# Inverse roots of two norms: one GpSimd power in place of a seed and ten operations

## The chip, the cores and the metric

The kernel runs on one core of a Trainium2 chip. The metric is the device time of one execution in microseconds, as the median of several runs. Beside the runs there is one profiled execution, from which all durations here come. A core has five engines with a queue each: PE (TensorE, matmuls and transposes; its weight loads are listed as PEld), DVE (VectorE), ACT (ScalarE), POOL (GpSimd) and SP, which only issues DMAs here. An engine executes its instructions in the order of its queue, and waits at an instruction until the work of other engines that it needs is done.

## The reference

The input x has 512 x 512 positions of 64 channels in fp32. Two layers of the same form follow each other, and each adds its result to x. Cut to what matters:

```python
def layer(x):                                   # twice, with weights of its own
    xn = _ln(_gn(x)) * norm_scale + norm_bias   # group norm, then layer norm, over 64 channels
    left  = (xn @ Wl + bl) * mask * sigmoid(xn @ Wlg + blg)      # 64 -> 128
    right = (xn @ Wr + br) * mask * sigmoid(xn @ Wrg + brg)
    out_gate = sigmoid(xn @ Wog + bog)
    out = _banded_ingoing(left, right, 4)       # each row: sum of 9 neighbouring rows, weighted by left
    out = _ln(out) * out_gate                   # layer norm over 128 channels, with scale and bias
    return x + out @ Wo + bo                    # 128 -> 64

def _ln(x, eps=1e-6):
    m, v = mean(x, axis=-1), var(x, axis=-1)
    return (x - m) / sqrt(v + eps)

def _gn(v, G=32, eps=1e-5):                     # mean and variance of 2 channels over all positions
    return (g - m) / sqrt(s + eps)
```

So there are three places where an inverse root 1/sqrt(v + eps) is needed: the inner layer norm (one number per position), the outer layer norm (one per position) and the group norm (one per group of channels, once a layer).

## The kernel before

The 512 rows are cut into 9 blocks of up to 64 rows, which overlap by the width of the band, and the columns into two halves of 256. The 128 partitions hold the 64 rows of a block for both halves. A chunk is 128 columns of each half; a layer has 9 x 2 = 18 chunks. A chunk is walked in 16 steps, in each of which one unit `z` of 8 columns per half enters, and, some 30 steps later, one unit `Out` leaves. `layer` (with its loop over `t`, the step) writes out by hand which engine does what in which order: everything that it calls through `en` is kept in program order on its engine, by the helper at line 373, and so nearly all instructions of the profile bear line 373.

What happens to a unit that enters: `load` fetches z; `affine` applies the group norm (two operations with `ga` and `gb`, on DVE for the first units of a layer, on POOL for the others); `inner_stats` takes mean and variance with bn_stats on DVE; `solve` makes the inverse root; `inner_norm` subtracts the mean and multiplies by the root `rs` (two operations on POOL); `transposed` turns z on PE, from where ACT copies it (`zT`); `right` and `right_gate`, `right_end` make the gated right product (PE, ACT's sigmoid `sg`, DVE's multiply into `RO`).

What happens to one that leaves: in the first ten steps of a chunk `mix` multiplies `RO` with the left matrix `A` (one or two mixes a step, each of 32 matmuls), and ACT and DVE copy the result back into `RO`; `out_stats` takes its statistics on DVE; `solve` makes the root; `norm` applies it on ACT (eight operations a step, with `rs` as scale and `nm` as bias); `turned`, `gates`, `times_gate` (DVE, into `ZH`) and `end` follow; `biased` adds the bias to the fetched x in `XR` on POOL, and `ended` adds the result and stores it. In the first layer `sums` gathers the statistics for the second layer's group norm.

`solve` is called once every four steps, for the inner norm of about four units and the outer norm of four others at once. DVE forms the variances of both in one tile `v` of up to 96 columns (in most solves 32 + 32), and the negative means `nm`; `rsqrt` makes the roots into `r`; two POOL operations multiply the outer roots by the mask and `nm` by the roots. `rsqrt(o, v, vec, e)` makes a seed on `vec` by treating the float's bits as an integer (one tensor_scalar into `o`), and refines it on `e` in two rounds: six and four operations, of which the profile shows the results as `rsqrt` (the two scratch tiles) and `rs` (`o`).

In the order of the step in which it runs, `solve` stands behind the step's `affine` and statistics and ahead of `right_end`, `biased` and `times_gate`. So on POOL it is followed by the XR addition of the same step and the z of the next; on DVE by the product that frees a pair of PSUM banks for PE.

The group norm's roots come from `group_affine`, which calls `rsqrt(ga, ve)` with both engines left at their default, DVE: once after the statistics of the input (`input_stats`), and once between the layers, at the end of `mid_stats`.

Of the kernel before, what the change touches and what calls it, by code (L numbers as in the profile page):

```python
# [8 lines left out]
F32 = mybir.dt.float32  # L9
I32 = mybir.dt.int32  # L10
AF = mybir.ActivationFunctionType
ALU = mybir.AluOpType
# [4 lines left out]
P = 128  # L17
# [11 lines left out]
NB = 32  # L29
# [50 lines left out]
def tile_two_banded_layers(  # L80
# [6 lines left out]
    nc = tc.nc  # L87
# [7 lines left out]
    const = ctx.enter_context(tc.tile_pool(name="const", bufs=1))  # L95
    sm = ctx.enter_context(tc.tile_pool(name="sm", bufs=2))
# [28 lines left out]
        same.rearrange("p (g t) -> p g t", t=2), last(pair, 2), 1.0 / (2.0 * L * L), None, ALU.mult  # L125
    )

    def one_bank():
        return ps.tile([P, 512], F32, tag="ps", name="bank")

    def two_banks():
        return ps2.tile([P, 1024], F32, tag="ps2", name="banks")

    def rsqrt(o: bass.AP, v: bass.AP, vec=nc.vector, e=nc.vector):


        p, n = v.shape
        t, u = (
            sm.tile([P, 3 * NB], F32, tag=f"rsqrt{i}", name="rsqrt", bufs=1)[:p, :n]
            for i in range(2)  # L140
        )
        vec.tensor_scalar(
            o.bitcast(I32), v.bitcast(I32), -0.5, float(0x5F3759DF), ALU.mult, ALU.add
        )
        e.tensor_tensor(t, o, o, ALU.mult)
        e.tensor_tensor(t, t, v, ALU.mult)
        e.tensor_scalar(u, t, -10.0 / 3.0, None, ALU.add)
        e.tensor_tensor(t, t, u, ALU.mult)
        e.tensor_scalar(t, t, 5.0, None, ALU.add)
        e.tensor_tensor(o, o, t, ALU.mult)  # L150
        e.tensor_tensor(t, o, o, ALU.mult)
        e.tensor_tensor(t, t, v, ALU.mult)
        e.tensor_scalar(t, t, -27.0 / 1024.0, 0.5625, ALU.mult, ALU.add)
        e.tensor_tensor(o, o, t, ALU.mult)


    PARTS = (
# [61 lines left out]
    def solve_layer(i: int, f: dict, r: dict, tmp, half: bass.AP):  # L219
# [9 lines left out]
        for nm, lo, hi in (("right", 0, 2), ("left", 2, 4), ("gate", 4, 5)):  # L229
            lo, hi = lo * H, hi * H  # L230
            pm = one_bank()[:, : hi - lo]
            nc.tensor.matmul(pm, lhsT=half, rhs=aug[:, lo:hi], start=True, stop=True)
            pb = one_bank()[:, : hi - lo]
            nc.tensor.matmul(pb, lhsT=hb, rhs=raw[:, lo:hi], start=True, stop=False)
            nc.tensor.matmul(pb, lhsT=ones_row, rhs=brow[:, lo:hi], start=False, stop=True)
            nc.vector.tensor_tensor(r[nm], aug[:, lo:hi], pm, ALU.subtract)
            nc.vector.tensor_tensor(r[nm], r[nm], pb, ALU.add)
# [14 lines left out]
        nc.vector.tensor_scalar(r["Wo"], f["wo"], osc, None, ALU.mult)  # L252

        pb = one_bank()
        nc.tensor.matmul(pb[:, :D], lhsT=ones_row, rhs=f["bo"], start=True, stop=True)
        add = r["add"].rearrange("p (t c) -> p t c", c=D)
# [51 lines left out]
    def group_affine(mean: bass.AP, var: bass.AP, pool):  # L308

        ve = pool.tile([P, D], F32, name="g_ve")  # L310
        nc.vector.tensor_scalar(ve, var, GN_EPS, None, ALU.add)
        rsqrt(ga, ve)
        nc.vector.scalar_tensor_tensor(gb, mean, -1.0, ga, ALU.mult, ALU.mult)
# [284 lines left out]
    def solve(w: dict, ins: list, outs: list, sti, sto):  # L598

        ni, no = len(ins) * JU, len(outs) * JU  # L600
        v = sm.tile([P, 3 * NB], F32, tag="var", name="var", bufs=1)[:, : ni + no]
        r = sm.tile([P, 3 * NB], F32, tag="rs", name="rs", bufs=3)[:, : ni + no]
        if ni:
            en.vector.tensor_scalar(
                v[:, :ni].rearrange("p (k t) -> p k t", t=2), sti[:, : ni // 2, 2::3],
                1.0 / D, LN_EPS, ALU.mult, ALU.add,
            )
            for n, u in enumerate(ins):
                u.rs = r[:, n * JU : (n + 1) * JU]
        if no:  # L610

            js = slice(outs[0].m, outs[0].m + no)
            vo = v[:, ni:]
            en.vector.scalar_tensor_tensor(
                vo.rearrange("p (k t) -> p k t", t=2), sto[:, :, 2::3], 1.0 / H,
                w["m2"][:, js].rearrange("p (k t) -> p k t", t=2), ALU.mult, ALU.mult,
            )
            en.vector.tensor_scalar(vo, vo, LN_EPS, None, ALU.add)
            nm = sm.tile([P, NB], F32, tag="nm", name="nm")[:, :no]
            en.vector.tensor_scalar(  # L620
                nm.rearrange("p (k t) -> p k t", t=2), sto[:, :, 1::3], -1.0, None, ALU.mult
            )
        rsqrt(r, v, en.vector, en.gpsimd)
        if no:
            ro = r[:, ni:]
            en.gpsimd.tensor_tensor(ro, ro, w["m"][:, js], ALU.mult)
            en.gpsimd.tensor_tensor(nm, nm, ro, ALU.mult)
            for n, o in enumerate(outs):
                o.rs, o.nm = ro[:, n * JU : (n + 1) * JU], nm[:, n * JU : (n + 1) * JU]
# [109 lines left out]
    def layer(src: bass.AP, dst: bass.AP, w: dict, stats: bool, then=None):  # L739
# [60 lines left out]
        for t in range(min(loads), last_t + 3):  # L800
# [59 lines left out]
            if t % 4 == 0:  # L860
                st, us = sti.pop((t + 4) // 4, (None, []))
                so, os = sto or (None, [])
                sto = None
                if us or os:
                    solve(w, us, os, st, so)
# [156 lines left out]
def build(arrays):  # L1022
    import concourse.bacc as _bacc

    nc = _bacc.Bacc("TRN2", target_bir_lowering=False, num_devices=1)
    aps = {}
    for name in _INS:
        a = arrays[f"in_{name}_dram"]
        aps[name] = nc.dram_tensor(
            f"in_{name}_dram", a.shape, mybir.dt.from_np(a.dtype), kind="ExternalInput"  # L1030
        ).ap()
    out = nc.dram_tensor("out_0_dram", aps["x"].shape, F32, kind="ExternalOutput").ap()
    layers = [{n: aps[f"L{i}_conv_{n}"] for n in _NAMES} for i in range(2)]
    with tile.TileContext(nc) as tc:
        tile_two_banded_layers(tc, aps["x"], layers, out)
    return nc
# [10 lines left out]
```

## Time and profile before

| | |
|---|---|
| runs | 4804.82, 4806.53, 4807.79 us; median 4806.53 us |
| profiled execution | 4808.51 us |
| its span, from the first to the last instruction | 4806.5 us |
| granted TensorE clock, mean | 0.948 of full speed |
| set-up and statistics of the input | 0 to about 300 us |
| first layer | about 300 to 2560 us |
| second layer | about 2560 to 4806 us |

A line of a group of instructions reads: source line, engine, operation, output<-inputs by the program's names, shapes, count; then busy time in us and mean ns of one; then the idle time of the engine just before these instructions, and what ended it. In the list of waits, "A <- B: total, times, longest" means that A's engine stood idle until B was done. A line of the timeline has start and duration in us, and in square brackets the idle time before it with what ended that. A line of a stretch has its bounds, its length and the busy time of each engine with the number of instructions.

### The profile page before, as it was taken

The page shows a single profiled execution, that of the slowest core. Times are in us where ns is not written, and L with a number is a line of the kernel's source. Part 1 is how long each engine was busy: PE and PEld are TensorE (multiplying, and loading weights), DVE is VectorE, ACT ScalarE, POOL GpSimd, SP SyncE. Part 2 cuts the span into 40 slices and gives each one's busy share as a digit, 9 for nine tenths or more (in the row PEclk, how much of TensorE's full clock was granted, in tenths as well). Part 3 has the DMA queues.
Part 4 walks back from the last instruction along what each step waited for, and adds up shares of the span by engine and source line. Part 5 has one row for each costly group of instructions (what it writes and reads, how often), then busy time and mean ns, then how long its engine had stood idle before and what let it go on. Part 6 is the DMA issues. An engine that isn't in the chain of part 4 may idle for free. (4 is left out here: it accounts for less than half of the span.)

```text
span 4806.5 us, 193543 instructions
## 1 busy us (share of the span) xinstructions
PE 3796.6 (79%) x76306; PEld 3293.0 (69%) x76306; DVE 3929.9 (82%) x9635; ACT 3708.4 (77%) x8732; POOL 3817.1 (79%) x4739
## 2 busy tenths in 40 slices
PE   1025799989999999999985478888888888888888
PEld 0024688878888887888854467777777777777775
DVE  6954788888888888888867478888888888888887
ACT  0013689888888898989883268888888888888899
POOL 0035999999999999999734589999999999999964
PEclk9997999999999999999997689999999999999999
DMA  7859677777777777777763967777777777777876
GB/s 299 336 178 108 172 212 213 215 210 215 211 209 210 211 214 212 214 212 215 199 170 100 105 168 212 216 214 209 217 213 215 213 213 218 210 216 211 222 200 179
DMA packets 1437651, 983.63 MB, mean 205 GB/s; under 512 B 167202, under 2 KB 1284424, under 8 KB 1432392
## 3 DMA queue, kind: packets, MB, share of 16 engines
q1 hardware_dynamic: 1432064, 969.75, 73.6%
q8 instruction: 604, 9.90, 0.9%
q14 instruction: 303, 2.48, 0.2%
q10 hardware_dynamic: 4680, 1.50, 0.1%
HBM read 658.42 MB, written 312.46 MB: 202 GB/s over the span
## 5 line engine op out<-in xcount | busy, mean ns | idle before, releaser
L373 ACT ACTIVATE on<-RO,nm,rs 128x128 f32<-128x128 f32 x4608 | 1927.7, 496 | 15.3 <-PE bank L373 9.9
L373 PEld LDWEIGHTS banks<-pack,zT 64*128 64x128 f32 x18576 | 1251.3, 195 | 549.5 <-ACT zT L373 288.9
L373 PE MATMUL banks<-pack,zT 64*128 64x128 f32 x18576 | 1365.6, 289 | 272.8 <-ACT zT L373 222.6
L373 DVE TENSOR_TENSOR RO<-banks,sg 128x512 f32<-128x512 f32 (+1 forms) x1188 | 795.3, 673 | 228.3 <-POOL sg L373 116.2
L373 DVE SCALAR_TENSOR_TENSOR ZH<-bank,pack,gate 128x448 f32<-128x448 f32 (+1 forms) x1152 | 741.6, 685 | 173.3 <-PE bank L373 97.3
L373 ACT ACTIVATE sg<-banks 128x512 f32<-128x512 f32 (+1 forms) x1188 | 698.0, 589 | 188.6 <-PE banks L373 188.2
L373 DVE BATCH_NORM_STATS2 sto<-RO 128x6 f32<-128x256 f32 x2304 | 800.8, 411 | 3.7
L373 POOL TENSOR_TENSOR z<-z,gb 128x512 f32<-128x512 f32 x536 | 684.8, 1278 | 42.0
L373 PE MATMUL bank<-RO,A 64*64 64x128 f32 x18432 | 706.0, 292 | 3.9 <-ACT RO L373 2.4
L373 PE MATMUL bank<-pack,ZH 128*64 128x64 f32 x18432 | 694.6, 231 | 5.0 <-ACT gate L373 4.1
L373 POOL TENSOR_TENSOR z<-z,ga 128x512 f32<-128x512 f32 x536 | 685.6, 1279 | 3.2 <-DMA z<-mid_x 1.9
L373 POOL TENSOR_TENSOR z<-z,rs 128x512 f32<-128x512 f32 x586 | 619.3, 1057 | 46.0
L373 DVE COPY RO<-bank 128x512 f32<-128x512 f32 x576 | 398.4, 692 | 310.6 <-PE bank L373 307.3
L373 PEld LDWEIGHTS bank<-pack,ZH 128*64 128x64 f32 x18432 | 612.6, 143 | 47.3 <-ACT gate L373 8.5
L373 POOL TENSOR_TENSOR z<-z,sti 128x512 f32<-128x512 f32 x586 | 627.9, 1072 | 0.0
L373 PEld LDWEIGHTS bank<-RO,A 64*64 64x64 f32 x18432 | 582.0, 142 | 43.0 <-ACT RO L373 4.1
L373 ACT ACTIVATE gate<-bank 128x448 f32<-128x448 f32 (+1 forms) x1152 | 565.8, 545 | 34.5 <-PE bank L373 32.0
L373 ACT ACTIVATE zT<-banks 128x512 f32<-128x512 f32 (+1 forms) x1084 | 463.5, 481 | 139.6 <-PE banks L373 128.9
L373 PE MATMUL bank<-zg,pack 64*128 64x448 f32 (+1 forms) x2304 | 564.3, 556 | 4.6 <-DMA zg<-later 4.6
L373 ACT COPY RO<-bank 128x512 f32<-128x512 f32 x576 | 333.2, 579 | 282.3 <-PE bank L373 282.1
L373 PE MATMUL banks<-ident,z 64*128 64x64 f32 x4336 | 254.1, 233 | 359.2 <-DVE RO L373 336.9
L373 DVE BATCH_NORM_STATS2 sti<-z 128x6 f32<-128x128 f32 x2344 | 500.5, 280 | 15.2 <-POOL z L373 14.2
(144 smaller groups left out, 3908.6 us busy)
## 6 DMA issues: line engine op xcount, KB each, us to landing
later<-zT SPq DMA_DIRECT2D x576, 256.0 KB
A<-left_of SPq DMA_DIRECT2D x1152, 128.0 KB
zg<-later SPq DMA_DIRECT2D x576, 256.0 KB
z<-in_x_dram SPq DMA_DIRECT2D x576, 128.0 KB
z<-mid_x SPq DMA_DIRECT2D x576, 128.0 KB
gn_x<-in_x_dram SPq DMA_DIRECT2D x16, 4096.0 KB
XR<-in_x_dram SPq DMA_DIRECT2D x448, 112.0 KB
mid_x<-XR SPq DMA_DIRECT2D x448, 112.0 KB
```

Of the source, the lines that this page charges most:

```text
L373: return lambda *a, **k: tc.keep_in_program_order(f(*a, **k))
```

## The change

`rsqrt` loses the seed, the ten operations and their two scratch tiles. In their place stands one POOL tensor_tensor with the power operator, whose second operand is a constant column of -0.5, stretched over all columns. The column is set up once by DVE. `solve` calls it with POOL as the engine; `group_affine`, whose code stays, now gets POOL by default, where it had DVE.

```diff
@@ -125,33 +125,20 @@
+    minus_half = const.tile([P, 1], F32, name="minus_half")
+    nc.vector.memset(minus_half, -0.5)
+
...
-    def rsqrt(o: bass.AP, v: bass.AP, vec=nc.vector, e=nc.vector):
+    def rsqrt(o: bass.AP, v: bass.AP, e=nc.gpsimd):
         p, n = v.shape
-        t, u = (
-            sm.tile([P, 3 * NB], F32, tag=f"rsqrt{i}", name="rsqrt", bufs=1)[:p, :n]
-            for i in range(2)
-        )
-        vec.tensor_scalar(
-            o.bitcast(I32), v.bitcast(I32), -0.5, float(0x5F3759DF), ALU.mult, ALU.add
-        )
-        e.tensor_tensor(t, o, o, ALU.mult)
-        e.tensor_tensor(t, t, v, ALU.mult)
-        e.tensor_scalar(u, t, -10.0 / 3.0, None, ALU.add)
-        e.tensor_tensor(t, t, u, ALU.mult)
-        e.tensor_scalar(t, t, 5.0, None, ALU.add)
-        e.tensor_tensor(o, o, t, ALU.mult)
-        e.tensor_tensor(t, o, o, ALU.mult)
-        e.tensor_tensor(t, t, v, ALU.mult)
-        e.tensor_scalar(t, t, -27.0 / 1024.0, 0.5625, ALU.mult, ALU.add)
-        e.tensor_tensor(o, o, t, ALU.mult)
+        e.tensor_tensor(o, v, minus_half[:p].broadcast_to([p, n]), ALU.pow)
@@ -620,7 +607,7 @@
-        rsqrt(r, v, en.vector, en.gpsimd)
+        rsqrt(r, v, en.gpsimd)
```

## The prediction

> **What bounds the kernel now.** First the busy shares of the whole span, then the busy time of stretches inside the second layer.
>
> ```profile
> PE 3796.6 (79%) x76306; PEld 3293.0 (69%) x76306; DVE 3929.9 (82%) x9635; ACT 3708.4 (77%) x8732; POOL 3817.1 (79%) x4739
> ```
>
> ```profile
> core 0: us, PE busy (x) PEld busy (x) DVE busy (x) ACT busy (x) POOL busy (x), PEclk, DMA share, GB/s
> 3500.00:3530.00 30.00, 24.65 (x484) 21.45 (x480) 26.79 (x68) 29.83 (x74) 26.17 (x33) 1.00 0.80 225
> 3530.00:3575.00 45.00, 38.25 (x838) 33.81 (x840) 40.81 (x95) 37.20 (x89) 42.28 (x54) 0.96 0.76 210
> ```
>
> The page alone would let no engine stand out. The stretches do: a chunk of 16 steps has six steps without mixing, where ACT is full (29.83 of 30.00), and ten with it, where POOL is (42.28 of 45.00, the rest being gaps between its small operations). So I went to POOL's groups, here from 3000 to 4400 us, where 49 solves run, 28.57 us apart:
>
> ```profile
> L373 POOL TENSOR_SCALAR rsqrt<-rsqrt 128x64 f32<-128x64 f32 x147 | 48.0, 326 | 12.9
> L373 POOL TENSOR_TENSOR rs<-rs,rsqrt 128x64 f32<-128x64 f32 x98 | 31.4, 321 | 8.2
> L373 POOL TENSOR_TENSOR rsqrt<-rsqrt,var 128x64 f32<-128x64 f32 x98 | 31.3, 320 | 7.7
> L373 POOL TENSOR_TENSOR rsqrt<-rs 128x64 f32<-128x64 f32 x98 | 28.7, 293 | 29.6 <-DVE rs L373 25.8
> L373 POOL TENSOR_TENSOR rsqrt<-rsqrt 128x64 f32<-128x64 f32 x49 | 15.7, 321 | 4.1
> ```
>
> These five groups are the ten operations of a root. Busy: 48.0 + 31.4 + 31.3 + 28.7 + 15.7 = 155.1 us, 3.17 us a solve. Idle before them: 62.5 us, of which 25.8 is a wait for DVE's seed and 36.7 (0.75 a solve) dispatch gaps. So the chain holds POOL for 3.91 us, and POOL's only true slack is the wait, whose size the two layers give (1000 to 2000 us with 34 solves, 3000 to 4400 us with 49):
>
> ```profile
> POOL rsqrt L373 <- DVE rs L373: 29.3, 34, 1.9
> ```
>
> ```profile
> POOL rsqrt L373 <- DVE rs L373: 25.8, 35, 1.7
> ```
>
> That is 0.86 us a solve in layer 1 and 0.53 in layer 2: POOL is occupied for 97% and 98% of these windows. It is the engine that the pace hangs on, and a late POOL also stretches DVE, as one solve in a mixing stretch shows (timeline of DVE, then of PE):
>
> ```profile
> 3558.04 1.01 DVE L373 TENSOR_SCALAR var<-sti 128x32 f32<-128x32 f32 x1
> 3558.98 0.18 DVE L373 SCALAR_TENSOR_TENSOR var<-sto,pack 128x32 f32<-128x32 f32 x1
> 3559.19 1.20 DVE L373 TENSOR_SCALAR var<-var 128x32 f32<-128x32 f32 x1
> 3560.31 0.17 DVE L373 TENSOR_SCALAR nm<-sto 128x32 f32<-128x32 f32 x1
> 3560.43 1.23 DVE L373 TENSOR_SCALAR rs<-var 128x64 int32<-128x64 int32 x1
> 3561.58 0.68 DVE L373 TENSOR_TENSOR RO<-banks,sg 128x512 f32<-128x512 f32 x1
> ...
> 3562.40 0.46 PE L373 MATMUL banks<-ident,z 64*128 64x64 f32 x8 [3.92 <-DVE RO L373]
> ```
>
> Three operations that take 0.16 to 0.20 us in a quiet solve take 1.0 to 1.2 here, while POOL runs 1.28 us operations back to back; the product RO comes late behind them, and PE waits 3.92 us for it.
>
> **The change, part by part.** The program has 160 solves: 128 of them 64 columns wide (64 a layer), 32 between 24 and 48 wide at the ends of the layers. From each go a DVE seed and ten POOL operations; one POOL power operation comes. POOL's other work keeps its order, and no DMA moves.
>
> *Removed from POOL:* 3.91 us a solve. *Removed from DVE:* the seed, 0.20 us undisturbed, up to 1.23 as above. While POOL sets the pace this gain is worth nothing by itself, since DVE then waits for POOL's z later; if POOL were relieved it would come out of PE's waits.
>
> *Added to POOL:* a power, D us for 64 columns, plus one gap (0.75/10 = 0.08). No row shows a power. Lower bound: one two-input operation of that shape, 0.32 us. Upper bound, an estimate: a power with a free exponent is a logarithm, a product and an exponential; I count some 10 terms for the first, 6 for the last, each a multiply-add, and as many steps again to split and join exponents and sort out special values, 32 to 40 steps. As instructions of their own these would cost 0.40 us each (0.32 and a gap), so 40 x 0.40 = 16 us. The nearest row is the chain itself, ten such steps in 3.91 us. Inside one instruction the gaps and some reading and writing fall away, so I take 32 steps at 0.24, the cheapest step of the chain: 7.7, rounded to D = 8 us. A step could be far cheaper with everything kept inside the cores; both ends stay in the range.
>
> [...]
>
> *Behind it on POOL* stand the two small products for rs and nm, then XR and all z of the next steps; for these wait ACT's norm, one step later, and PE's transposes. With POOL already full, each microsecond beyond what is removed and the slack lengthens the solve's period:
>
> - layer 1: 64 x (8 + 0.08 - 3.91 - 0.86) = 64 x 3.31 = 212 us
> - layer 2: 64 x (8 + 0.08 - 3.91 - 0.53) = 64 x 3.64 = 233 us
> - the 32 narrower solves lie where POOL is idle much of the time (185.34 us busy of 260 from 300 to 560 us, 96.97 of 206 in the last stretch): 0; without that cover, half of D against 3.3 us, 32 x 0.8 = 26 us.
>
> A power holds POOL for long; could it hold DVE's small operations as the z operations do? The next of these are a period later and need z that POOL scales after the power, so they can't meet it: 0.
>
> *Group norm.* Its two roots, so far on DVE, become a power on POOL between two DVE operations. The first is covered: DVE waits 47.2 us for zeros to land before XR is cleared. The second is bare, at the seam of the layers:
>
> ```profile
> 2563.90 0.20 DVE L142 TENSOR_SCALAR ga<-on 128x64 int32<-128x64 int32 x1
> ...
> 2566.62 0.22 DVE L313 SCALAR_TENSOR_TENSOR gb<-on,ga 128x64 f32<-128x64 f32 x1
> ```
>
> Seed to gb takes 2.72 us; the power takes 8 and two hand-overs at 0.08 (seed's end to POOL's start at 3506.06): + 5.4 us. The constant's memset is one column on DVE during set-up, under 0.1 us, beside the loads.
>
> Sum: 212 + 233 + 5 = 450 us onto the span of 4806.5 (its execution 4808.5, the median of the runs 4806.53): **5257 us**. D from 6 to 11 gives 5000 to 5640, the own range of this case.
>
> **Rivals.** *A cheap power (faster).* The point that decides is D = 4.4 to 4.7 us, where the formulas cross zero. For it speaks that ten trips through memory become one; against it, the count of steps. What it would give: PE's transposes start 7.17 us apart in undisturbed steps with two mixes, 6.23 with one, 5.69 with none; the chunk from 3530.34 to 3643.98 has 6, 4 and 6 of them, 102 us undisturbed against 113.6 measured. So some 11 us a chunk, 18 chunks a layer: 200 us in layer 2; layer 1's same reckoning from 1491.62 to 1558.43 gives 7.8 a chunk, 140. All of it would be 4470; D of 1 to 2.5 frees 3 to 1.5 us a solve and brings perhaps 60%: **4600 us**. Chance 0.33.
>
> *A very dear power.* If the cores work their partitions one after another, D is 16 us and more: 64 x (11.31 + 11.64) = 1469, narrower solves 32 x 4.7 = 150, the seam 13: **6440 us** and up without end, as POOL has no cover left. Against it: each POOL row shows 128 partitions at 1.6 ns a column ((1043 - 320)/448). Chance 0.10.
>
> *Nothing happens.* D within about 0.1 us of the crossing, or the freed POOL time turns into ACT's bound, which six steps a chunk already have: **4806 us**. Chance 0.03; that the program is not what it says is excluded, since its queues hold one power a solve.
>
> **How the numbers follow.** The forecast has 0.54, the rivals 0.33, 0.10 and 0.03. No change is within 0.2% (10 us), about what a measurement of this kernel can tell. Slower: 0.54 + 0.10. The range runs from 4560, which leaves out the best part of the cheap case, to 6400, which leaves out the dear one.
>
> **What would show it.** A group rs<-var,minus_half of 128 operations at 128x64 and its mean, counted start to start: near 8 us my D holds, under 4.4 the first rival. POOL's wait for DVE before it should vanish and POOL be full in all stretches, with ACT's non-mixing steps longer than 5.69 us. Wrong would be a long power with little lost time, or a short one with PE waiting as before.

## The result, and the profile after

The changed kernel takes 5629.52 us (four runs, 5627.82 to 5631.06), the kernel before on the same chip 4805.67 us: ratio 1.1716, 95% interval 1.1695 to 1.1736. It is 17% slower; the forecast was 5257 us, within a range of 4560 to 6400. The page of the profiled execution opens with the busy shares:

```profile
PE 4045.0 (72%) x76306; PEld 3479.2 (62%) x76306; DVE 3916.1 (70%) x9454; ACT 3750.1 (67%) x8732; POOL 4875.8 (87%) x3301
```

POOL has 1438 instructions fewer than before and 1059 us more to do. DVE and ACT have hardly more, so their shares fall. (PE has the same number of matmuls, with 248 us more of busy time, at a mean granted clock of 0.889 instead of 0.948. That clock did not set the time here: of four executions of run 11 below, two had a clock of 0.87 and two of 0.89, and their times lie within 2.1 us of each other.) One stretch in each layer shows what is full:

```profile
core 0: us, PE busy (x) PEld busy (x) DVE busy (x) ACT busy (x) POOL busy (x), PEclk, DMA share, GB/s
1000.00:2000.00 1000.00, 806.02 (x16076) 703.78 (x16076) 722.10 (x1727) 747.47 (x1727) 970.77 (x665) 0.91 0.63 176
4000.00:4700.00 700.00, 524.47 (x9994) 457.31 (x9994) 504.79 (x1212) 512.53 (x1205) 678.91 (x461) 0.88 0.63 176
```

POOL is at 97%, and the gaps between its operations make up most of the rest. The groups of POOL's instructions hold what stands for the ten operations of the root:

```profile
L360 POOL TENSOR_TENSOR rs<-var,minus_half 128x64 f32<-128x64 f32 x128 | 1348.4, 10535 | 45.4 <-DVE nm L360 34.7 <-DVE var L360 9.0
...
L360 POOL TENSOR_TENSOR rs<-var,minus_half 128x32 f32<-128x32 f32 x22 | 119.3, 5424 | 100.6 <-DVE nm L360 95.9 <-DVE var L360 4.7
```

A power of 64 columns takes 10.53 us where the chain took 3.91, and one of 32 columns 5.42: 0.16 us a column. What stands behind it is seen in the timeline around one of them (all engines; lines left out between):

```profile
3996.93 10.53 POOL L360 TENSOR_TENSOR rs<-var,minus_half 128x64 f32<-128x64 f32 x1
...
4007.86 0.25 POOL L360 TENSOR_TENSOR nm<-nm,rs 128x32 f32<-128x32 f32 x1
4008.07 1.18 POOL L360 TENSOR_TENSOR XR<-XR,pack 120x512 f32<-120x512 f32 x1
4008.14 1.66 ACT L360 ACTIVATE on<-RO,nm,rs 128x128 f32<-128x128 f32 x4 [6.28 <-POOL nm L360]
...
4009.28 0.69 DVE L360 TENSOR_TENSOR XR<-bank,XR 120x512 f32<-120x512 f32 x1 [5.38 <-POOL XR L360]
...
4010.03 1.97 PE L360 MATMUL bank<-RO,A 64*64 64x128 f32 x28 [4.92 <-DVE XR L360]
```

ACT stands 6.28 us for the root, DVE 5.38 us for the XR sum behind it in POOL's queue, and PE 4.92 us for a bank that DVE frees late. Such waits are among the longest of the whole span:

```profile
ACT on L360 <- POOL nm L360: 614.7, 137, 8.9
...
DVE XR L360 <- POOL XR L360: 518.8, 131, 8.0
```

POOL's own wait for DVE, 29.3 us between 1000 and 2000 us before, has shrunk to 6.2 in the same window:

```profile
L360 POOL TENSOR_TENSOR rs<-var,minus_half 128x64 f32<-128x64 f32 x28 | 295.0, 10535 | 6.7 <-DVE nm L360 3.4 <-DVE var L360 2.8
```

### The profile page after: what moved, and what is told of

It is laid out like the page before. It is cut to its first block, busy times and chain, and to the rows that moved or that the text cites. A ratio compares the mean times of both kernels' runs of the same rounds, so it can differ in the third digit from the quotient of the medians.

```text
span 5629.0 us, 191928 instructions
## 1 busy us (share of the span) xinstructions
PE 4045.0 (72%) x76306; PEld 3479.2 (62%) x76306; DVE 3916.1 (70%) x9454; ACT 3750.1 (67%) x8732; POOL 4875.8 (87%) x3301
## 5 line engine op out<-in xcount | busy, mean ns | idle before, releaser
L360 ACT ACTIVATE on<-RO,nm,rs 128x128 f32<-128x128 f32 x4608 | 1920.3, 492 | 640.0 <-POOL nm L360 614.7
L360 PEld LDWEIGHTS banks<-pack,zT 64*128 64x128 f32 x18576 | 1372.5, 213 | 933.3 <-ACT zT L360 627.8
L360 PE MATMUL banks<-pack,zT 64*128 64x128 f32 x18576 | 1491.0, 307 | 611.4 <-ACT zT L360 569.6
L360 POOL TENSOR_TENSOR rs<-var,minus_half 128x64 f32<-128x64 f32 (+4 forms) x160 | 1535.8, 9599 | 197.0 <-DVE nm L360 141.9
L360 PE MATMUL bank<-RO,A 64*64 64x128 f32 x18432 | 751.5, 299 | 183.1 <-DVE XR L360 172.9
L360 DVE TENSOR_TENSOR XR<-bank,XR 120x512 f32<-120x512 f32 (+1 forms) x576 | 395.8, 687 | 563.3 <-POOL XR L360 518.8
L360 PEld LDWEIGHTS bank<-RO,A 64*64 64x64 f32 x18432 | 610.6, 146 | 236.6 <-DVE XR L360 183.3
L360 PE MATMUL bank<-zg,pack 64*128 64x448 f32 (+1 forms) x2304 | 628.6, 615 | 3.4 <-DMA zg<-later 3.4
L360 DVE COPY RO<-bank 128x512 f32<-128x512 f32 x576 | 397.5, 690 | 322.0 <-PE bank L360 319.1
L360 DVE BATCH_NORM_STATS2 sti<-z 128x6 f32<-128x128 f32 x2344 | 504.5, 281 | 124.6 <-POOL z L360 121.9
```

The lines of the kernel that those rows point to most:

```text
L360: return lambda *a, **k: tc.keep_in_program_order(f(*a, **k))
```

## The experiments

The runs of one group (1 to 4, 5 to 8, 9 to 11) share a chip and its runs of the kernel before (medians 4831.88, 4827.48 and 4837.55 us), so they are read by their ratio to it; "+121" means the ratio less one, times the 4806.5 us of the first trace.

**1. What a root for nearly nothing would bring.** The changed kernel's power becomes a multiplication:

```diff
-        e.tensor_tensor(o, v, minus_half[:p].broadcast_to([p, n]), ALU.pow)
+        e.tensor_tensor(o, v, minus_half[:p].broadcast_to([p, n]), ALU.mult)
```

> The changed kernel with a multiplication in the place of the power, on the same operands and at the same places of POOL's queue; the roots themselves are left out. Theory (POOL's occupancy sets the pace on both sides): one operation of about 0.32 us and a gap instead of 3.91 us, 3.5 us freed a solve, of which ACT and PE let 60 to 90% through: 4500 to 4680 us. Rival (POOL was only just full, and other engines take over at once when it is relieved): 4790 to 4810 us.

4721.20 us, ratio 0.9772 (0.9756 to 0.9788): -110 us. The gain is there, so POOL did set the pace, but it is a quarter of the 450 us of POOL time that are freed (3.5 x 128), and less than my 4600 for a cheap power. Both theories miss: POOL was the fullest engine, but the next were close behind (before, from 3000 to 4400 us: POOL busy for 93%, DVE for 89, ACT for 88). In the second layer (3000 to 4400 us) of this run:

```profile
3000.00:4400.00 1400.00, 1192.78 (x24810) 1041.30 (x24812) 1238.94 (x2998) 1260.64 (x3003) 1192.32 (x1154) 0.98 0.79 219
```

```profile
POOL XR L360 <- DMA XR<-mid_x: 124.3, 73, 5.7
```

ACT (fourth) is now at 90%, DVE at 88 and POOL at 85; and POOL, running ahead, stands 124 us for the fetch of x.

**2. Half the power.** In the changed kernel's `rsqrt`:

```diff
-        e.tensor_tensor(o, v, minus_half[:p].broadcast_to([p, n]), ALU.pow)
+        h = n // 2
+        e.tensor_tensor(o[:, :h], v[:, :h], minus_half[:p].broadcast_to([p, h]), ALU.pow)
+        e.tensor_tensor(
+            o[:, h:], v[:, h:], minus_half[:p].broadcast_to([p, n - h]), ALU.mult
+        )
```

> The power on the first half of the columns, a multiplication on the second half, whose roots are left out. Theory (occupancy, 0.16 us a column): 5.42 + 0.25 and two gaps, 5.83 us in place of 3.91: 64 x (5.83 - 3.91 - 0.86) + 64 x (5.83 - 3.91 - 0.53) = 157 us, the seam 3: 4966 us, 4930 to 5010. Rival (what costs is the lateness of the root for ACT, which before the change began 1.7 us after the end of the chain, so that the first 1.7 us are free): 64 x 2 x (5.83 - 3.91 - 1.7) = 28 us: 4825 to 4845.

4953.13 us, ratio 1.0252 (1.0237 to 1.0268): +121, against 160 by occupancy and 28 by the rival. The first stands, 40 us too high. Two rows tell most of why, POOL's group here and its wait for the seed over the whole span before:

```profile
L364 POOL TENSOR_TENSOR rs<-var,minus_half 128x32 f32<-128x32 f32 x256 | 722.1, 2837 | 11.4 <-DVE var L364 7.5
```

```profile
L373 POOL TENSOR_TENSOR rsqrt<-rs 128x64 f32<-128x64 f32 x256 | 74.9, 293 | 111.6 <-DVE rs L373 101.6
```

The two operations hold POOL for (722.1 + 3.9)/128 = 5.67 us a solve, not 5.83, and the slack is 101.6 us in all, where the two windows gave 64 x (0.86 + 0.53) = 89. With both, and the 7.5 us of waiting that are left, the wide solves come to 128 x (5.67 - 3.91) - 101.6 + 7.5 = 131 us.

**3. XR out of the power's way.** In the changed kernel's step, `biased` moves ahead of `solve`:

```diff
+            if t in outs:
+                biased(outs[t], w, stats)
             if t % 4 == 0:
                 st, us = sti.pop((t + 4) // 4, (None, []))
...
-            if t in outs:
-                biased(outs[t], w, stats)
```

> The changed kernel with the step's XR addition ahead of the power in POOL's queue instead of behind it. Theory (occupancy; the waits of DVE for XR, 519 us in the trace, only show where a full POOL makes others wait): 5590 to 5650 us, the wait moves to other lines. Rival (the long instruction hurts by standing ahead of XR, on which DVE and then PE hang): most of the 519 us come back, 5100 to 5300 us.

5658.69 us, ratio 1.1713 (1.1696 to 1.1731), the same as the changed kernel's 1.1716 (5630 us as the first chip would have it, inside the expected range). DVE's 519 us of waiting for XR are gone from the head of the list, and other waits have grown in their place (these three were 614.7, 319.1 and 121.9 us in the changed kernel):

```profile
ACT on L360 <- POOL nm L360: 699.3, 142, 10.1
DVE RO L360 <- PE bank L360: 428.7, 460, 9.9
...
DVE sti L360 <- POOL z L360: 319.1, 119, 8.5
```

The wait for XR named a victim, not the cause.

**4. A power that nobody waits for.** The kernel before keeps its roots and gets an extra power:

```diff
+    idle = const.tile([P, 2 * NB], F32, name="idle")
...
             if t in outs:
                 biased(outs[t], w, stats)
+            if t in outs and t in units and t % 4 == 0:
+                en.gpsimd.tensor_tensor(
+                    idle, all_ones[:, : 2 * NB], minus_half.broadcast_to([P, 2 * NB]), ALU.pow
+                )
```

> The kernel before with its seed and ten operations, and an extra power of 64 columns whose result nobody reads, behind the XR addition of every fourth step (64 a layer). Theory (occupancy): 64 x (10.61 - 0.86) + 64 x (10.61 - 0.53) = 1269 us more: 6075 us, 5980 to 6130. Rival (the lateness of the roots costs, not POOL's time): nothing waits for this result, 4806 to 4850 us.

6094.72 us, ratio 1.2616 (1.2597 to 1.2635): +1257 us where 1269 were worked out. Its group and POOL's remaining wait for the seed, between 1000 and 2000 us:

```profile
L377 POOL TENSOR_TENSOR idle<-all_ones,minus_half 128x64 f32<-128x64 f32 x26 | 274.6, 10561 | 0.0
...
L377 POOL TENSOR_TENSOR rsqrt<-rs 128x64 f32<-128x64 f32 x50 | 14.7, 294 | 7.9 <-DVE rs L377 6.0
```

No root is later for its own sake here, and the time is lost all the same. With runs 2 and 3 this settles that POOL's occupancy is what costs, not the lateness of the root or the long instruction's place ahead of XR.

**5. What a power's price depends on.** During set-up, in the kernel before:

```diff
+        for power in (-0.5, 2.0, 1.0):
...
+            for p, n in ((P, 64), (P, 8), (P, 128), (16, 64), (4, 64)):
+                tc.keep_in_program_order(
+                    nc.gpsimd.tensor_tensor(
+                        probe[:p, :n], base[:p, :n], ex[:p].broadcast_to([p, n]), ALU.pow
+                    )
+                )
...
```

> The kernel before, with powers of several shapes and exponents on POOL in the set-up, where POOL has nothing to do (2 to 228 us), results unread. Theory (one pass of the same code for each column, all partitions side by side, nothing depends on the values; 0.31 us and 0.16 a column by the widths of the changed kernel): 128x8 1.6 us, 128x64 10.5, 128x128 20.8, and 16x64 and 4x64 10.5 too, the same for exponents 2 and 1 and for a base of 1. Rival (partitions one after another): 4x64 about a quarter of 16x64. Rival (short ways for easy exponents): 2 and 1 far under 10.5. The kernel's time is that of before, 4806 to 4835 us.

4834.62 us in a single run, and 4827.48 before (4822.43 to 4834.08). From POOL's groups (base 1.5; L971 has the base 1.0):

```profile
L965 POOL TENSOR_TENSOR probe<-base,ex-0.5_108 128x128 f32<-128x128 f32 x1 | 20.7, 20727 | 0.1
...
L965 POOL TENSOR_TENSOR probe<-base,ex2.0_115 128x64 f32<-128x64 f32 x1 | 10.5, 10517 | 0.1
...
L971 POOL TENSOR_TENSOR probe<-base,ex1.0_122 128x64 f32<-128x64 f32 x1 | 10.5, 10517 | 0.1
...
L965 POOL TENSOR_TENSOR probe<-base,ex2.0_115 4x64 f32<-4x64 f32 x1 | 10.5, 10506 | 0.1
...
L965 POOL TENSOR_TENSOR probe<-base,ex-0.5_108 128x8 f32<-128x8 f32 x1 | 1.6, 1646 | 0.0
```

Twice the columns cost twice the time ((20.73 - 1.65)/120 = 0.159 us a column, 0.37 for the instruction). Four partitions cost what 16 and 128 do (10.51 to 10.73 us at 64 columns), so the partitions are not taken one after another. An exponent of 1 or 2 or a base of 1 is no cheaper. Both rivals fall.

**6. The power for the group norm alone:** in `group_affine`,

```diff
-        rsqrt(ga, ve)
+        nc.gpsimd.tensor_tensor(ga, ve, minus_half.broadcast_to([P, D]), ALU.pow)
```

> The kernel before with the power for the group norm's two roots alone; solve keeps its seed and ten operations. Theory: the first is hidden, the second adds 10.53 + 0.16 - 2.72 = 8.0 us at the seam of the layers: ratio 1.0010 to 1.0022. Rival (neither is hidden): 16 us, 1.0033; rival (the seam hides it too): 1.0000.

4829.87 us, ratio 1.0004 (0.9995 to 1.0012): between my 8 us and nothing. The trace of before tells why, in a line that I had not read: 10 us behind the roots DVE stood for the loads of z,

```profile
2577.36 0.69 DVE L373 TENSOR_TENSOR z<-z,ga 128x512 f32<-128x512 f32 x1 [3.63 <-DMA z<-mid_x]
```

and this wait is gone where the power delays DVE, so that it covers 3.6 of the 8 us. The 4.4 that are left lie inside the interval, and the traces of this chip show them: from POOL's 73rd root to its 81st, across the seam, it is 211.6 us in run 5 and 216.0 here.

**7. Eight operations in place of ten.** If POOL's time is what counts, a shorter iteration should pay. Two Newton rounds with constants fitted to them, and a seed constant to match:

```diff
-            o.bitcast(I32), v.bitcast(I32), -0.5, float(0x5F3759DF), ALU.mult, ALU.add
+            o.bitcast(I32), v.bitcast(I32), -0.5, float(0x5F376908), ALU.mult, ALU.add
...
+        for top in (1.50087896, 1.50000057):
+            e.tensor_tensor(t, o, o, ALU.mult)
+            e.tensor_tensor(t, t, v, ALU.mult)
+            e.tensor_scalar(t, t, -0.5, top, ALU.mult, ALU.add)
+            e.tensor_tensor(o, o, t, ALU.mult)
```

> The kernel before with two rounds of Newton's iteration in place of a cubic round and a Newton round: eight POOL operations instead of ten, seed and constants fitted to it. Theory (POOL sets the pace, and a part of what is freed comes through): 0.79 us freed in 128 solves is 101 us, of which a quarter (as in the run with a multiplication, 110 of 450) to all comes: 25 to 100 us faster, ratio 0.979 to 0.995. Rival (the ten-operation kernel has enough slack): 0.998 to 1.002.

4757.64 us, ratio 0.9864 (0.9845 to 0.9882): -65 us, faster than both kernels. The relief is larger than the 0.79 us expected: a root's eight operations take 2.94 us from start to end, 0.97 less than the ten. The ten have two tensor_scalars with one operator, at 0.37 us each, which this run does without; its own have two operators and take 0.24 (the group of this run, then the two with one operator in run 8):

```profile
L365 POOL TENSOR_SCALAR rsqrt<-rsqrt 128x64 f32<-128x64 f32 x256 | 62.7, 245 | 22.4
```

```profile
L369 POOL TENSOR_SCALAR rsqrt<-rsqrt 128x64 f32<-128x64 f32 x256 | 94.3, 368 | 22.4
```

**8. Six operations,** the second round of the kernel before left out, so that the roots are not complete:

> The kernel before without the second round of the root (six POOL operations instead of ten, the last refinement left out). Theory (the first microseconds that are freed come through, then another engine or a DMA sets the pace): 1.57 us freed a solve, 60 to 105 us faster, most of the 110 us that the multiplication brought. Rival (gain in proportion to what is freed): 110 x 1.57/3.5 = 49 us.

4756.03 us, ratio 0.9854 (0.9839 to 0.9869): -70 us. The six operations take 2.41 us, a relief of 1.50; that is half as much again as in run 7 and brings hardly more, so the gain is not in proportion, and the first microsecond of POOL time is worth most.

**9 and 10. The fetch of x earlier,** since run 1 left POOL waiting for it; once with the multiplication, once with the eight operations:

```diff
-            if t + 1 in outs:
-                fetch(src, outs[t + 1], w, t + 1)
...
+            if t + 2 in outs:
+                fetch(src, outs[t + 2], w, t + 2)
             if t - 1 in outs:
                 ended(dst, outs[t - 1])
```

> The run with a multiplication in the power's place (roots left out), and the fetch of x for the result half a step to a step earlier: two steps ahead, in SP's queue ahead of the previous result's store instead of behind it. Theory (with POOL relieved, the late fetch of XR, for which POOL waits 124 us of 1400 in layer 2, keeps back a part of the gain): 30 to 100 us under the 4721 of that run, ratio to before 0.957 to 0.971. Rival (these waits are POOL's slack, and PE and ACT, 92 and 90% busy, set the pace): within 15 us of it, 0.974 to 0.980.

4704.14 us, ratio 0.9734 (0.9716 to 0.9753), 0.0038 under run 1, or 18 us: between both expectations. POOL's wait for the fetch halves, but another, for DVE, comes up beside it, from 17.4 us in run 1 (3000 to 4400 us):

```profile
POOL rs L360 <- DVE nm L360: 65.7, 30, 4.4
POOL XR L360 <- DMA XR<-mid_x: 65.3, 41, 4.4
```

So most of this waiting is slack of a POOL that is no longer the bound. (Run 1 ran on another chip, so the 18 us rest on the two ratios.) What bounds then (ACT at 91% and PE at 86 in that window, PE at 92 in layer 1) was not taken apart further.

> The kernel with eight POOL operations a root, and the same earlier fetch. Theory (POOL waits for the fetch 3 us of 1000 and 16 of 1400 there, so little is to be had): ratio to before 0.980 to 0.988. Rival (a fetch ahead of the store is worth a step's latency everywhere): under 0.975.

4753.17 us, ratio 0.9827 (0.9814 to 0.9841): the fastest version that computes everything, 1.7% under the kernel before. How much of the step from run 7 is the fetch stays open, as the runs come from two chips and the intervals lie only 0.0004 apart.

**11. The power in `solve` alone,** with the group norm's roots on DVE as before:

> The changed kernel with the group norm's two roots by seed and ten operations on DVE as before; the power in solve alone. Theory (all but a few microseconds of the loss is solve's): ratio to before 1.169 to 1.172, 3 to 10 us under the changed kernel. Rival (the seam of the layers carries tens of microseconds): under 1.165.

5649.84 us, ratio 1.1680 (1.1664 to 1.1696): it lies below the expected 1.169 to 1.172, but the interval reaches into it and just touches the whole change's. By the ratios 17 us of the loss are not `solve`'s, by the traces fewer: from the 73rd root to the 81st it is 221.7 us with the whole change and 218.3 here, so that the seam's share is 3.4 us. Nearly all the loss is `solve`'s.

## Why the prediction was right, and by how much not

**What bounds: right.** POOL's occupancy, 97 to 98% of the stretches before, set the pace, and what was added to it came out as time nearly one to one. The runs, ordered by POOL's time for a root:

| run | POOL per solve, against 3.91 us | time |
|---|---|---|
| 1, multiplication | -3.5 us | -110 us |
| 8, six operations | -1.50 | -70 |
| 7, eight operations | -0.97 | -65 |
| 2, half power | +1.76 | +121 |
| the change | +6.6 | +825 |
| 4, chain and power | +10.6 | +1257 |

Upwards the slope is that of a bound engine, near 128 us for each us: from the change's wide solves alone, which lose 783 us (below), to run 4, whose narrow solves are as before, it is (1257 - 783)/(10.6 - 6.6) = 118. Downwards it flattens at once. Run 1 also leaves out DVE's seed, which runs 7 and 8 keep; how much of its further gain is the seed's was not separated.

**The price of the power: too small.** This is the term that was mis-sized: D was taken as 8 us, 32 steps at 0.24, and is 10.53. At the price I gave a step that would be 44 steps. What a power is made of and the count of its steps were an estimate of mine that no row showed and no run shows; the runs show the 10.53 us as a whole. So it was luck that D lay on the right side of the 4.4 to 4.7 us that decide between faster and slower. The sum as put, with 10.53, is 64 x 5.84 + 64 x 6.17 = 769 us for the wide solves and 8 for the seam, 5583 us. Solve by solve, the start of POOL's first root operation in both traces:

| solve | before, us | after, us | behind by |
|---|---|---|---|
| 9th, first wide one of layer 1 | 529.40 | 537.46 | 8.1 |
| 73rd, first narrow one after them | 2375.58 | 2766.25 | 390.7 |
| 81st, first of layer 2 | 2586.26 | 2987.96 | 401.7 |
| 89th, first wide one | 2817.32 | 3227.83 | 410.5 |
| 153rd, first narrow one after them | 4644.71 | 5455.33 | 810.6 |
| 160th, last | 4779.55 | 5599.39 | 819.8 |

The wide solves of layer 1 lose 390.7 - 8.1 = 383 us, those of layer 2 400: 5.98 and 6.25 us each, where the terms at the true D say 5.84 and 6.17. So the slack in the wait for the seed was about right, in part by errors that cancel: 101.6 us of it were there and not 89, and of POOL's waiting before a wide power 43.7 us are left, where none was expected.

**The narrow solves: not free.** They were put at 0, as POOL is idle for 29% of the first stretch and 53% of the last (96.99 us busy, not 96.97). The table gives 11 us before the ninth (it starts 3.2 us earlier than before at the first, and is 8.1 behind by then), 11 between 73rd and 81st with the seam, 9 before the 89th and 9 after the 153rd: some 36 us without the seam's 4.4. At 32 columns a power is 5.42 us against 3.28, at 40 columns 6.75 against 3.43, at 48 columns 8.00 against 3.97, at 24 columns 4.53 against 4.27. For the 22, 4, 4 and 2 such solves that is 77 us, so about half of it shows. The share of idle time in a stretch was half a cover. That the work behind waits for these roots is the likely reason; no run takes them apart.

**The seam:** 8 us by the term, of which a wait for z's loads, which the trace of before held, covers 3.6 (run 6). The first group norm's power was hidden, as said: DVE waits for a DMA in both kernels, 47.2 us before and 38.0 after.

**The power did not hold DVE:** put at 0, and the runs need nothing for it: run 4's sum closes within 12 us of 1269. DVE's products beside a power keep their 0.68 us, and in run 5 a tensor_scalar of 640 columns in the set-up takes 0.47 us beside a power, as it does before without one.

**The rivals.** The cheap power was refuted by its price, 10.53 us against the 4.4 to 4.7 that decide. My value for it was also off: 4600, or 206 us, where run 1 with a lower price still than was put there brings 110. The reckoning from undisturbed steps took every long step as POOL's doing, 340 us in all, of which it then took 60%. The dear power, partitions one after another, was refuted by run 5 (10.51 to 10.73 us for 64 columns on 4, 16 and 128 partitions).

## What to carry to other kernels

One instruction in place of eleven is no gain by itself: what counted here is how long the engine is held (10.53 us against 3.91), and the length of an instruction that no trace has shown is to be measured in an idle corner of a kernel before it is built in. On an engine that was occupied to 98% (busy time and gaps), an addition could be worked out as count times excess, less the wait that it had left (run 4: 1269 us worked out, 1257 measured); a relief could not, as the next engine was near (run 1: 110 of 450 us came through, with ACT then at 90%). A list of waits says who suffers: moving the victim away from the long instruction changed nothing (run 3: ratio 1.1713 against 1.1716), while two operations fewer on the full engine paid at once (run 7: 65 us).

## What the hardware showed that I had not expected

A power on POOL cost 0.159 us a column of fp32 and 0.37 us for the instruction in run 5 (1.65 us for 8 columns, 10.56 for 64, 20.73 for 128, with exponent -0.5), the same within some 2% for 4, 16 and 128 partitions, for exponents -0.5, 1 and 2 and for bases 1.5 and 1.0. A two-input multiplication of 64 columns there took 0.29 to 0.32 us in the kernel before, so a power of 64 columns, 10.53 us in the changed kernel, is worth 33 to 36 of them. A tensor_scalar of 64 columns there took 0.37 us with one operator (run 8) and 0.24 with two (run 7).
